# Attention within a chunk: scores from the diagonal on, the blocks left of it by transposing

## The chip, the cores and the metric

The kernel runs on one core of one Trainium2 chip. A core has a matrix engine (TensorE, PE in the profile; PEld is its weight load), a vector engine (VectorE, DVE), an engine for activation functions (ScalarE, ACT), a general one (GpSimd, POOL), and SyncE (SP), which issues transfers. They run side by side, each works through its own queue in order, and semaphores join them. The metric is the device time of one execution in microseconds, as the median of several runs.

## The reference

The program computes two layers on an input of 2 x 128 x 64 x 64. The first layer is a group norm, a neighbourhood attention and three linear layers. The second takes the image as 4096 tokens of 128 channels and adds an attention of the normalised tokens with themselves, and then a spectral filter layer. The change is in the attention of the second layer. Cut to what matters:

```python
def _L1_attn_ref(q):                       # q: 2 x 4096 x 128, the layer-normed tokens
    scale = 1.0 / np.sqrt(128)
    sim = jnp.einsum('blh,bmh->blm', q, q) * scale
    sim = jnp.where(eye, -1e9, sim)        # a token doesn't see itself
    attn = jax.nn.softmax(sim, axis=-1)
    return jnp.einsum('blm,bmh->blh', attn, q)

t = t + _L1_attn_ref(_ln_t(t))
```

Queries, keys and values are the same tensor, so the matrix of scores is symmetric, and so is the matrix of its exponentials, since no row maximum is taken off. Everything is in fp32.

## The kernel before, in words

Up to about 346 us the first layer runs. Then come the two batches of the second layer's attention, one after the other, and from about 1306 us the filter layer.

For a batch, `attention(b, fill)` (L882) divides the 4096 tokens into 8 chunks of 512, each of them four tiles of 128 tokens. `cm[b]` holds the normalised tokens with the channels on the partitions, `tok[b]` the same with the tokens on the partitions. Because of the symmetry only the 36 pairs of chunks (a, c) with c at or behind a are computed (`pairs`, L892). For a pair, `weights(a, c, k)` (L895) makes four tiles `e`, one for each tile k of chunk a, of 128 x 512 exponentials: one matmul into a PSUM bank (L899), in a diagonal pair (a = c) an addition of -1e6 on the diagonal of the tile's own 128 x 128 block by VectorE (L904), and the exponential on ScalarE (L906), which also writes the row sums to `part[:, n, c]`.

A tile e of a pair off the diagonal is used twice. As it stands it is the moving operand of a product with `tok` that adds to the output of chunk c (`other`, L952). And `turned` (L909) transposes its blocks, four to a bank (L913), and a VectorE instruction (L916) copies the bank to SBUF as `et` and sums its rows into `part[:, n, a]`; `et` is the moving operand of the product for chunk a (`own`, L927). In a diagonal pair the four tiles hold the full 512 x 512 square of exponentials, both of its triangles computed from scores, and only `own` is fed, with e itself.

The main loop (L938) goes through the pairs. In the four steps of a pair it issues the scores of the following pair (`weights(*following, j)`), the products of this one, one late product with an `et`, and one portion of other work by `fill()`: the end of the first layer, the token preparation of the second batch, filters, and for a finished chunk `after` (L969: transposing back, dividing by the sum over `part`, layer norm and the transform products L1012 and L1022) and `short_lags` (L1036, with L1053). In the second batch `fill()` also loads and mixes the filter matrices (`filter_matrices`, L1121; its loads of `st` land in two buffers, L1112, and VectorE consumes them at L1117 and L1119). The first scores of a batch (L937) are issued ahead of the loop, with no product between them.

Buffers around the change: PSUM has eight banks; `own` and `other` take one each, and six are handed out in turn by `bank()` (L865) for scores, transposes and fill work alike. Tiles `e` have eight buffers, tiles `et` four, `part` one.

What sets the order: each engine's queue is in order. Inside the blocks `with tc.manual_schedule(...)` (the first layer on four engines, the filter layer on PE) the order is as written. The attention stands in no such block, so there the framework's planner puts each engine's instructions in order: by the order of the program, and by when it expects inputs and buffers to be ready. A PE instruction whose input isn't there holds up everything behind it on PE.

Of the kernel before, what the change touches and what calls it, by code (L numbers as in the profile page):

```python
# [8 lines left out]
F32 = mybir.dt.float32  # L9
AF = mybir.ActivationFunctionType  # L10
ALU = mybir.AluOpType
# [3 lines left out]
P = 128  # L15
# [3 lines left out]
NT = T // P  # L19
# [8 lines left out]
ASCALE = P ** -0.5  # L28
# [58 lines left out]
CHUNKS = (0, 1, 4, 5, 2, 3, 6, 7)  # L87
# [8 lines left out]
def kernel(  # L96
# [16 lines left out]
    nc = tc.nc  # L113
# [18 lines left out]
    tt, tok, cm = [None, None], [None, None], [None, None]  # L132
# [11 lines left out]
    ident = const.tile([P, P], F32, name="ident")  # L144
# [79 lines left out]
    with l0a:  # L224
# [6 lines left out]
        sp = l0a.enter_context(tc.tile_pool(name="l0_s", bufs=2))  # L231
# [626 lines left out]
    with ap_:  # L858
        tp = ap_.enter_context(tc.tile_pool(name="l1_t", bufs=1, side="right"))
        ep = ap_.enter_context(tc.tile_pool(name="l1_e", bufs=8, side="right"))  # L860
        sp = ap_.enter_context(tc.tile_pool(name="l1_s", bufs=2, side="right"))
# [3 lines left out]
        def bank():  # L865
            return ps_m.tile([P, 512], F32, tag="bank", name="bank")
# [7 lines left out]
        one = tp.tile([P, 512], F32, name="one")  # L874
# [7 lines left out]
        def attention(b, fill):  # L882

            part = sp.tile([P, NT, 8], F32, tag="part", name="part", bufs=1)
            pairs = [(a, c) for a in range(8) for c in range(a, 8)]  # L892
            chunk = lambda a: slice(CHUNKS[a] * 512, (CHUNKS[a] + 1) * 512)

            def weights(a, c, k):  # L895

                n = 4 * CHUNKS[a] + k
                ps = bank()
                nc.tensor.matmul(  # L899
                    ps, lhsT=cm[b][:, n * P : (n + 1) * P], rhs=cm[b][:, chunk(c)], start=True, stop=True  # L900
                )
                if a == c:
                    ks = slice(k * P, (k + 1) * P)
                    nc.vector.tensor_tensor(ps[:, ks], ps[:, ks], ndiag, ALU.add)  # L904
                e = ep.tile([P, 512], F32, tag="e", name="e")
                nc.scalar.activation(e, ps, AF.Exp, bias=0.0, scale=ASCALE, accum_out=part[:, n, c : c + 1])  # L906
                return e

            def turned(a, c, m, es):  # L909

                pt = bank()
                for k in range(4):
                    nc.tensor.transpose(pt[:, k * P : (k + 1) * P], es[k][:, m * P : (m + 1) * P], ident)  # L913
                et = ep.tile([P, 512], F32, tag="et", name="et", bufs=4)
                n = 4 * CHUNKS[c] + m
                nc.vector.tensor_tensor_reduce(  # L916
                    et, pt, one, 1.0, 0.0, ALU.mult, ALU.add, part[:, n, a : a + 1]
                )
                return et

            own = None

            def onto(a, n, e, first, last):
                nonlocal own
                if first:
                    own = ps_o.tile([P, 512], F32, tag="own", name="own")
                nc.tensor.matmul(own, lhsT=tok[b][:, n, :], rhs=e, start=first, stop=last)  # L927
                if last:
                    xs = xa[b][:, chunk(a)]
                    if a:  # L930
                        nc.vector.tensor_tensor(xs, own, xs, ALU.add)
                    else:
                        nc.vector.tensor_copy(xs, own)
                    fill(CHUNKS[a], part)

            late = []
            es = [weights(0, 0, k) for k in range(4)]  # L937
            for i, (a, c) in enumerate(pairs):  # L938
                following = pairs[i + 1] if i + 1 < len(pairs) else None
                coming = []  # L940
                if a != c:
                    other = ps_o.tile([P, 512], F32, tag="other", name="other")
                for k in range(0, 4, 2):
                    for j in (k, k + 1):
                        if following:
                            coming.append(weights(*following, j))
                        if a == c:
                            while late:
                                onto(*late.pop(0))
                            onto(a, 4 * CHUNKS[a] + j, es[j], j == 0, a == 7 and j == 3)  # L950
                        else:
                            nc.tensor.matmul(  # L952
                                other, lhsT=tok[b][:, 4 * CHUNKS[a] + j, :], rhs=es[j], start=(j == 0), stop=(j == 3)
                            )
                        if late:
                            onto(*late.pop(0))
                        fill()
                    if a != c:
                        for j in (k, k + 1):
                            late.append((a, 4 * CHUNKS[c] + j, turned(a, c, j, es), False, c == 7 and j == 3))  # L960
                if a != c:
                    xs = xa[b][:, chunk(c)]
                    if a:
                        nc.vector.tensor_tensor(xs, other, xs, ALU.add)
                    else:
                        nc.vector.tensor_copy(xs, other)
                es = coming
# [223 lines left out]
        def filler(b, steps, kept=None):  # L1191

            urgent, done = [], []

            def fill(c=None, part=None):
                if c is not None:
                    done.append(c)
                    urgent.append(after(b, c, part))
                    if len(done) % 4 == 0:
                        held = kept if kept is not None and len(done) == 4 else urgent  # L1200
                        held.append(short_lags(b, len(done) // 4 - 1))
                    return

                for queue in (urgent, steps):
                    while queue:
                        got = next(queue[0], False)
                        if got is None:
                            return
                        if got:
                            break  # L1210
                        queue.pop(0)

            return fill, urgent
# [17 lines left out]
        steps = [drain(), chosen, filters(), tokens(1, bank)]  # L1231
        fill, left = filler(0, steps)
        attention(0, fill)
        for gen in steps:
            for _ in gen:
# [30 lines left out]
        kept = []  # L1266
        fill, left = filler(1, steps, kept)
        attention(1, fill)
        for gen in steps:
            for _ in gen:  # L1270
# [18 lines left out]
    with ExitStack() as cv:  # L1289
# [17 lines left out]
        def group():  # L1307


            y = cp.tile([P, 8, KF, 2, 32], F32, tag="y", name="y", bufs=2)  # L1310
            for q in range(GB // 2):
                ct, ut = ahead.pop(0)
                for par in range(2):

                    cv_ = ct[:, :, 0 : 288 + par * 32].rearrange("p o (l c) -> p o l c", l=2)[:, :, :, 0 : FB * KF]
                    for b in range(NB):
                        for f in range(2):
                            fp = slice(f * 64, (f + 1) * 64)
                            pc = ps_c.tile([P, 2, 2, FB * KF], F32, tag="pc", name="pc")
                            nc.tensor.matmul(pc, lhsT=ut[fp, b, par, :], rhs=cv_[fp], start=True, stop=True)  # L1320
                            (nc.scalar.copy if f else nc.vector.tensor_copy)(  # L1321
                                y[:, 4 * f : 4 * f + 4, :, par, b * 2 * FB + q : (b + 1) * 2 * FB : 2],
                                pc.rearrange("p r l (t k) -> p (r l) k t", k=KF),
                            )
                if to_load:
                    q_ = to_load.pop(0)
                    ahead.append((blocks(q_), inputs(q_)))
            return y
# [34 lines left out]
        with tc.manual_schedule(engines={mybir.EngineType.PE}):  # L1363
            y = group()
            for g in range(BINS // GB):
                following = group() if g + 1 < BINS // GB else None
# [17 lines left out]
        for b in range(NB):  # L1384
            for par in range(2):
                pt = ps_c.tile([P, 4, P], F32, tag="pc", name="pt")
# [5 lines left out]
        for h in range(2):  # L1392
            for b in range(NB):
                o = cp.tile([P, P, FB, 2], F32, tag="o", name="o", bufs=2)
                for par in range(2):
# [4 lines left out]
                    for i in range(4):  # L1400
                        for q, py in ((0, odd), (1, even)):
# [3 lines left out]
                                start=(q == 0), stop=(q == 0 or i == 3),  # L1405
# [102 lines left out]
```

## Time and profile before

| what | value |
|---|---|
| median of 3 runs | 2209.53 us (2209.5 to 2211.03) |
| profiled execution | 2211.93 us, its span 2210.2 us |
| PE busy | 2156.2 us, 98% of the span |
| DVE, ACT, POOL busy | 938.0, 780.6, 278.5 us |
| scores, L899 | 576 records, 297.9 us busy |
| exponentials, L906 | 288, 171.8 us busy, 597 ns each |
| transposes of e, L913 | 896 records, 117.2 us busy |
| copies with row sums, L916 | 224, 145.5 us busy, 687 ns each |
| diagonal additions, L904 | 64, 300 ns each (median) |

A fp32 matmul appears as two records on PE, each with a weight load; a transpose as one. A record's length runs into that of the next, since matmuls are pipelined, so what a matmul costs is read from start to start. In a row of the timeline stand the start, the length, the engine, the line, the operation, output and inputs, the shapes, how many records are merged, and in square brackets how long the engine was idle before it and what ended that.

### The profile page before, as it was taken

What the parts mean: (1) busy time and instruction counts of PE and PEld (TensorE: products, weight loads), DVE (VectorE), ACT (ScalarE), POOL (GpSimd) and SP (SyncE); (2) the same over time, 40 slices, a digit from 0 to 9 for tenths busy, and PEclk for the clock granted to TensorE, in tenths of its full rate; (3) what the DMA queues carried; (4) which work ended last, traced back from release to release, by engine and by line L of the source; (5) the groups of instructions that cost most, each with busy time, mean ns of one, the idle gap of its engine ahead of it and who ended that gap; (6) DMA issues with size and microseconds to landing.
All of it is one profiled execution on the core that took longest, in us unless ns stands there. A gap on an engine that the chain in (4) does not pass through costs nothing.

```text
span 2210.2 us, 31763 instructions
## 1 busy us (share of the span) xinstructions
PE 2156.2 (98%) x11920; PEld 1335.0 (60%) x11920; DVE 938.0 (42%) x3054; ACT 780.6 (35%) x1904; POOL 278.5 (13%) x355
## 2 busy tenths in 40 slices
PE   7899998999999998999999999999999999999998
PEld 4677765544554444544544447767767676777776
DVE  5899985434443346433333442232222323232232
ACT  3898883222333222222223232232222323232232
POOL 3477874200000000000000000000000000000000
PEclk8999999999999999999999999999999999999999
DMA  4222212021000025000000141221212121212101
GB/s 147 61 62 61 62 50 52 0 77 43 24 24 25 24 68 156 24 25 24 0 25 24 48 111 40 59 52 47 59 44 55 43 56 43 57 42 57 40 10 77
DMA packets 170345, 110.54 MB, mean 50 GB/s; under 512 B 21311, under 2 KB 155087, under 8 KB 169680
## 3 DMA queue, kind: packets, MB, share of 16 engines
q1 hardware_dynamic: 169266, 105.01, 17.8%
q8 instruction: 94, 1.54, 0.3%
q0 software_dynamic: 576, 2.10, 0.3%
q10 hardware_dynamic: 350, 1.41, 0.3%
q14 instruction: 59, 0.48, 0.1%
HBM read 73.86 MB, written 34.63 MB: 49 GB/s over the span
## 4 chain that ended last, share of the span: by engine, by line
PE 88%; DVE 5%; POOL 3%; DMA 2%; ACT 1%; issue 1%; SPq 1%; POOLq 0%; DVEq 0%; ACTq 0%
PE acc L1332 25%; PE pc L1320 13%; PE own L927 11%; PE bank L899 11%; PE other L952 8%; PE bank L913 4%; PE bank L333 2%; PE bank L1053 2%; PE bank L193 1%; PE bank L543 1%; PE bank L1012 1%; PE py L1354 1%; PE bank L507 1%; DMA st<-in_m_minus_dram 1%; PE po L565 1%; DVE ln_st L379 1%
## 5 line engine op out<-in xcount | busy, mean ns | idle before, releaser
L1321 DVE COPY y<-pc 128x512 f32<-128x512 f32 x320 | 221.6, 692 | 351.5 <-PE pc L1320 347.8
L906 ACT ACTIVATE e<-bank 128x512 f32<-128x512 f32 x288 | 171.8, 597 | 516.2 <-PE bank L899 387.8
L899 PE MATMUL bank<-cm 128*128 128x512 f32 x576 | 297.9, 601 | 1.4 <-DVE y L654 1.4
L1332 PE MATMUL acc<-y,mpl 128*128 128x256 f32 x1280 | 292.1, 382 | 0.0
L1332 PE MATMUL acc<-y,mmi 128*128 128x256 f32 x1280 | 288.0, 379 | 0.0
L1320 PE MATMUL pc<-ct,ut 64*128 64x512 f32 x1280 | 285.2, 595 | 0.9 <-issue 0.9
L1332 PEld LDWEIGHTS acc<-y,mpl 128*128 128x128 f32 x1280 | 238.1, 190 | 59.4 <-issue 29.6
L1332 PEld LDWEIGHTS acc<-y,mmi 128*128 128x128 f32 x1280 | 242.6, 190 | 32.6
L927 PE MATMUL own<-et,tok 128*128 128x512 f32 x448 | 228.5, 597 | 7.5 <-DVE part L916 7.4
L1321 ACT COPY y<-pc 128x512 f32<-128x512 f32 x320 | 205.1, 641 | 86.6 <-PE pc L1320 86.6
L952 PE MATMUL other<-e,tok 128*128 128x512 f32 x448 | 229.7, 594 | 0.0
L1320 PEld LDWEIGHTS pc<-ct,ut 64*128 64x128 f32 x1280 | 121.5, 187 | 145.8 <-issue 140.6
L916 DVE CUSTOM_DVE_ANT_0 et<-bank,one 128x512 f32<-128x512 f32 x224 | 145.5, 687 | 131.5 <-PE bank L913 131.4
L1339 ACT COPY ob<-acc 128x256 f32<-128x256 f32 x32 | 19.0, 595 | 387.0 <-PE acc L1332 387.0
L927 PEld LDWEIGHTS own<-et,tok 128*128 128x128 f32 x448 | 84.4, 191 | 117.5 <-issue 73.3
L952 PEld LDWEIGHTS other<-e,tok 128*128 128x128 f32 x448 | 85.2, 191 | 107.8 <-issue 106.0
L1356 DVE TENSOR_TENSOR xa<-py,xa 128x512 f32<-128x512 f32 x32 | 22.1, 692 | 281.4 <-PE py L1354 281.4
L913 PEld LDWEIGHTS bank<-ident,e 128*128 128x128 f32 x896 | 102.9, 141 | 55.4 <-issue 47.0
L899 PEld LDWEIGHTS bank<-cm 128*128 128x128 f32 x576 | 94.5, 191 | 67.9 <-issue 44.7
L165 POOL TENSOR_TENSOR ln_rs<-ln_rs,mhalf 128x4 f32<-128x4 f32 x24 | 24.5, 1020 | 837.1 <-DVE ln_rs L164 837.1
L530 ACT ACTIVATE p<-p,mn 128x196 f32<-128x196 f32 x256 | 114.4, 449 | 14.3 <-DVE mn L520 13.8
L913 PE MATMUL bank<-ident,e 128*128 128x128 f32 x896 | 117.2, 274 | 0.0
(210 smaller groups left out, 2289.3 us busy)
## 6 DMA issues: line engine op xcount, KB each, us to landing
ut<-us SPq DMA_DIRECT2D x80, 256.0 KB
us<-ub SPq DMA_DIRECT2D x64, 256.0 KB
vw<-vd SPq DMA_DIRECT2D x256, 49.0 KB
ct<-gs SPq DMA_DIRECT2D x160, 72.0 KB
ct<-gs SPq DMA_DIRECT2D x160, 64.0 KB
gs<-sum SPq DMA_DIRECT2D x20, 256.0 KB
vd<-v SPq DMA_DIRECT2D x128, 32.0 KB
st<-in_m_plus_dram SPq DMA_DIRECT2D x16, 256.0 KB
```

Source lines behind the costliest of these rows:

```text
L333: nc.tensor.matmul(pl, lhsT=wg[:, lo : lo + P], rhs=zT, start=True, stop=True)
L530: nc.scalar.activation(p, p, AF.Exp, bias=t[name + "mn"][:, h : h + 1], scale=-1.0, accum_out=t["den"][:, u, h : h + 1],)
L899: nc.tensor.matmul(ps, lhsT=cm[b][:, n * P : (n + 1) * P], rhs=cm[b][:, chunk(c)], start=True, stop=True)
L906: nc.scalar.activation(e, ps, AF.Exp, bias=0.0, scale=ASCALE, accum_out=part[:, n, c : c + 1])
L913: nc.tensor.transpose(pt[:, k * P : (k + 1) * P], es[k][:, m * P : (m + 1) * P], ident)
L916: nc.vector.tensor_tensor_reduce(et, pt, one, 1.0, 0.0, ALU.mult, ALU.add, part[:, n, a : a + 1])
L927: nc.tensor.matmul(own, lhsT=tok[b][:, n, :], rhs=e, start=first, stop=last)
L952: nc.tensor.matmul(other, lhsT=tok[b][:, 4 * CHUNKS[a] + j, :], rhs=es[j], start=(j == 0), stop=(j == 3))
L1053: nc.tensor.matmul(py, lhsT=mu[:, lag, :], rhs=zc[:, from_par, s0 : s0 + 512], start=(lag == 0), stop=(lag == 2))
L1320: nc.tensor.matmul(pc, lhsT=ut[fp, b, par, :], rhs=cv_[fp], start=True, stop=True)
L1321: (nc.scalar.copy if f else nc.vector.tensor_copy)(y[:, 4 * f : 4 * f + 4, :, par, b * 2 * FB + q : (b + 1) * 2 * FB : 2], pc.rearrange("p ...
L1332: nc.tensor.matmul(acc, lhsT=(mmi if l else mpl)[:, k, :], rhs=y[:, 1::2, k, ::-1, :] if l else y[:, 0::2, k, :, :], start=(l == 0 and k = ...
```

## The change

In a diagonal pair, the tile for k = 1, 2, 3 gets scores only from its own 128 x 128 block to the right: the matmul, the exponential and its row sum start at column `lo` = 128 k. The blocks left of it are the transposes of blocks that the pair's earlier tiles hold (`left`, the list of tiles made so far): k PE transposes into another bank, and one VectorE instruction copies them into e[:, 0:lo] and sums their rows into a ninth column of `part`, which is cleared once a batch by GpSimd. For k = 0 nothing changes but the size of `part`. Pairs off the diagonal stay as they were. Both callers hand over the list.

```diff
-            part = sp.tile([P, NT, 8], F32, tag="part", name="part", bufs=1)
+            part = sp.tile([P, NT, 9], F32, tag="part", name="part", bufs=1)
+            nc.gpsimd.memset(part[:, :, 8:9], 0.0)
             pairs = [(a, c) for a in range(8) for c in range(a, 8)]
...
-            def weights(a, c, k):
+            def weights(a, c, k, left=()):
 
                 n = 4 * CHUNKS[a] + k
+                lo = k * P if a == c else 0
                 ps = bank()
                 nc.tensor.matmul(
-                    ps, lhsT=cm[b][:, n * P : (n + 1) * P], rhs=cm[b][:, chunk(c)], start=True, stop=True
+                    ps[:, lo:], lhsT=cm[b][:, n * P : (n + 1) * P],
+                    rhs=cm[b][:, CHUNKS[c] * 512 + lo : (CHUNKS[c] + 1) * 512], start=True, stop=True,
                 )
                 if a == c:
                     ks = slice(k * P, (k + 1) * P)
                     nc.vector.tensor_tensor(ps[:, ks], ps[:, ks], ndiag, ALU.add)
                 e = ep.tile([P, 512], F32, tag="e", name="e")
-                nc.scalar.activation(e, ps, AF.Exp, bias=0.0, scale=ASCALE, accum_out=part[:, n, c : c + 1])
+                nc.scalar.activation(
+                    e[:, lo:], ps[:, lo:], AF.Exp, bias=0.0, scale=ASCALE, accum_out=part[:, n, c : c + 1]
+                )
+                if lo:
+                    pt = bank()
+                    for j in range(k):
+                        nc.tensor.transpose(pt[:, j * P : (j + 1) * P], left[j][:, lo : lo + P], ident)
+                    nc.vector.tensor_tensor_reduce(
+                        e[:, 0:lo], pt[:, 0:lo], one[:, 0:lo], 1.0, 0.0, ALU.mult, ALU.add, part[:, n, 8:9]
+                    )
                 return e
...
-            es = [weights(0, 0, k) for k in range(4)]
+            es = []
+            for k in range(4):
+                es.append(weights(0, 0, k, es))
...
-                            coming.append(weights(*following, j))
+                            coming.append(weights(*following, j, coming))
```

## The prediction

> **What bounds the kernel now.** I read the page's chain of waits first, then busy time by stretch over the attention, then the timeline of one step on the diagonal, then the rows that price the operations.
>
> The chain of waits:
>
> ```profile
> PE 88%; DVE 5%; POOL 3%; DMA 2%; ACT 1%; issue 1%; SPq 1%; POOLq 0%; DVEq 0%; ACTq 0%
> ```
>
> The end is set by TensorE (PE) nearly everywhere. Where it isn't shows in the busy time of PE, weight load, VectorE (DVE), ScalarE (ACT) and GpSimd (POOL) by stretch, with granted clock, DMA share and GB/s behind:
>
> ```profile
> 346.50:367.20 20.70, 18.87 (x61) 9.39 (x61) 12.93 (x60) 8.19 (x23) 15.46 (x18) 1.00 0.54 70
> 367.20:812.00 444.80, 443.64 (x1540) 219.00 (x1541) 182.65 (x612) 127.73 (x332) 29.30 (x32) 1.00 0.10 30
> 812.00:882.00 70.00, 62.44 (x201) 28.15 (x200) 46.81 (x128) 18.78 (x48) 2.31 (x2) 0.95 0.56 155
> 882.00:1260.00 378.00, 378.00 (x1271) 185.58 (x1270) 138.19 (x413) 102.35 (x276) 6.04 (x6) 1.00 0.09 25
> ```
>
> In 367 to 812 and 882 to 1260 PE is busy throughout and the chain names hardly anything but PE, so PE work saved there comes off the time. The first stretch (first batch starts) and the third (second batch starts) are different: the chain runs over transfers and DVE, e.g. these two pieces of it (start, length):
>
> ```profile
> 350.76 2.54 DMA st<-in_m_u_dram
> ...
> 818.51 3.23 DMA st<-in_m_plus_dram
> ```
>
> Each batch has eight diagonal pairs. By the times of the diagonal's DVE addition (L904), the first pair of each batch (348 and 818 us) lies in such a stretch, the other fourteen in the two PE stretches.
>
> One step on a diagonal, second batch, timeline (start, length):
>
> ```profile
> 1011.69 1.02 PE L899 MATMUL bank<-cm 128*128 128x512 f32 x2
> 1012.55 1.02 PE L952 MATMUL other<-e,tok 128*128 128x512 f32 x2
> 1012.75 0.30 DVE L904 TENSOR_TENSOR bank<-bank,ndiag 128x128 f32<-128x128 f32 x1
> 1013.14 0.60 ACT L906 ACTIVATE e<-bank 128x512 f32<-128x512 f32 x1 [3.10 <-DVE bank L904]
> 1013.41 1.02 PE L927 MATMUL own<-et,tok 128*128 128x512 f32 x2
> 1014.27 1.02 PE L899 MATMUL bank<-cm 128*128 128x512 f32 x2
> 1016.84 1.04 PE L913 MATMUL bank<-ident,e 128*128 128x128 f32 x8
> 1017.72 1.02 PE L899 MATMUL bank<-cm 128*128 128x512 f32 x2
> ```
>
> A fp32 product is two records. Start to start one of 512 columns takes 0.86 us (1011.69 to 1012.55); eight transposes take 0.88 (1016.84 to 1017.72). The e of the step is ready at 1013.74, 1.19 us after its score matmul's slot ended at 1012.55: 0.20 to DVE, 0.30 the addition, 0.09 to ACT, 0.60 the exponential.
>
> [...] here a 128-column transpose is 0.109 us and a 128-column product 0.222 (below), twice, and I use these. [...] L904 shows 0.30, used here.
>
> **The change part by part.**
>
> *Narrower scores.* Rows k = 1, 2, 3 of a diagonal pair compute 384, 256, 128 columns in place of 512. For 128 columns the nearest rows are the projection's four products, for 256 the later filter stage's 64 records of the chain:
>
> ```profile
> 355.67 1.05 PE L602 MATMUL bank<-w_sb,att 128*128 128x128 f32 x8
> 356.56 1.02 PE L899 MATMUL bank<-cm 128*128 128x512 f32 x2
> ...
> 1320.33 14.01 PE acc L1332 x64
> ```
>
> 0.89 / 4 = 0.222 us for 128 columns; 2 x 14.01 / 64 = 0.438 for 256; between them and 0.859, 0.648 for 384. Saved: 0.211 + 0.421 + 0.637 = 1.27 us a pair.
>
> *Turned left blocks.* 0 + 1 + 2 + 3 = 6 transposes at 0.109 = 0.66 us a pair. A lone transpose (k = 1) has no row of its own[...]. I take 0.109. Net on PE: 1.27 - 0.66 = 0.61 us a pair, and 14 x 0.61 = 8.6 us in the PE stretches.
>
> *ACT* loses 768 columns a pair. L906 at 512 is 0.597 us and ACT's 256-column copy (L1028) 0.374, so 0.87 ns a column: 0.67 us a pair, 11 in all, worth nothing while PE binds. It does bring e earlier.
>
> *DVE* gains three copies with sums a pair. L904's 0.30 at 128 and 0.687 of L916 at 512 give 0.30, 0.43, 0.56, plus three accumulator reads of 0.083: 1.54 us a pair, 24.6 in all. In the PE stretches DVE is busy 183 of 445 and 138 of 378 us, so this fits in idle time; the blocks are needed only when the diagonal's own products start, at least four score steps later. If that cover went (the addition of the next row late behind such a copy), ACT and then the transposes would be late.
>
> *The new wait.* The transposes of row k wait for e of row k - 1, and everything behind them on PE (products, fill work, later scores, thus ACT) waits too. In the fourteen pairs the gap from the end of an exponential to the next score matmul's start is 0.27 us at the least, typically 0.5 or 1.4 by turns, twice -0.04 (row 0 to row 1); the narrower matmul itself (0.65, 0.44, 0.22) comes before the transposes, so 0.6 us remain in nearly every case, against some 0.1 for the semaphore. Wait: nil, unless the order changes.
>
> *Banks.* Three more PSUM banks a pair from the six. One lives about 1 us (transposes, 0.2, copy), a score bank about 2, and a step lasts 2.6: room for both. Taken as nil; with fill work holding two more banks, up to 0.8 us a pair in the two pairs with transform products (7 and 15).
>
> *Memset* of the ninth column: one GpSimd instruction. It stands behind the 0.12 us memset of `zc` ahead of the first exponential (348.8), and at the second batch POOL is idle until 815. The row sums read 36 elements for 32. Both nil (at most 0.2).
>
> *The two first pairs.* PE savings don't count there; DVE additions may. First batch: DVE sits in the chain at 349.4 to 353.4, idle 0.96 and 0.68 us waiting for transfers. The first copy (0.38) with its wait falls before the instructions that free the next transfer's buffer, the rest into idle time: +0.8 us (0 to 1.6). Second batch: the same with the loads of m_plus, 1.48 us of idle DVE at 820 to 822: +0.5 (0 to 1.5).
>
> Sum: -8.6 + 0.8 + 0.5 = -7.3 us. The profiled execution took 2211.9 us (span 2210.2): 2204.6. The median of the runs is 2.4 below it; taking the same difference there, 2209.5 - 7.3 = 2202.2 us. The filter stage behind is PE throughout (877.5 of 878.2 us), so the shift is carried to the end.
>
> **Rivals.**
>
> *A. The gain is half lost in small waits* (banks, lone transposes, late DVE at the two starts): 0.25 a pair for 14 pairs, and 2.5 rather than 1.3 at the starts: -8.6 + 3.5 + 2.5 = -2.6, 2206.9. For it: DVE's copies stand between other work in a strict queue. Against: the slack above.
>
> *B. The transposes really wait: slower.* At both starts PE runs the four score matmuls in a row. If the order puts those of a pair so close in all fourteen, e of row 0 comes 1.29 us after its matmul (the 1.19 and 0.1 for the semaphore), with 0.65 covered: 0.64 lost; row 1's e is then in time; row 2's comes 1.07 after its matmul (addition, 256-column exponential), with 0.44 covered: 0.6 lost less the first transposes, say 0.4. Waits 1.05 against 0.61 gained: +0.44 a pair, +6.2, with the starts +7.5: 2217.0. It decides from a mean wait of 0.52 us a pair (no gain left). Against: two products separate the scores in all fourteen now, and PE's order here isn't written out but planned.
>
> *C. More is gained.* At the second start PE idles 4.42 us and then runs at half clock (two records 1.70 us apart from the next, not 0.86):
>
> ```profile
> 841.93 2.07 PE L927 MATMUL own<-et,tok 128*128 128x512 f32 x2 [4.42 <-DVE part L916]
> 844.65 1.91 PE L899 MATMUL bank<-cm 128*128 128x512 f32 x2
> 846.35 1.78 PE L952 MATMUL other<-e,tok 128*128 128x512 f32 x2
> ```
>
> This hangs on where DVE's queue stands, which the new copies shift. Without this wait some 6 us more: 2196. With it doubled, the gain would be gone.
>
> *D. It doesn't do what it says:* narrow products bound by their weight load. Two loads of 0.19 us for 128 columns, 0.38 and not 0.222, cost 0.16 a pair, 2.2 us: 2204.4. L602 speaks against it.
>
> **How the numbers follow.** Forecast with D's size: 0.60 (2199.5 to 2205); A 0.17; B 0.10; C 0.13. A difference under 0.2% (4.4 us) can't be told from none. Faster by more (below 2205.1): 0.60 + 0.12 = 0.72; slower (above 2213.9): 0.10; the same: 0.18. The range leaves out B, the edge of C and little of A: 2197 to 2210.
>
> **What would show it.** L899 in the diagonal pairs with three more forms, 8.6 to 10 us less start-to-start time in all; 96 transposes more from the new line, spaced 0.109; 48 copies of 0.30 to 0.56 us on DVE, 25 us with reads; no idle PE in front of the new transposes; the two PE stretches 4.3 us shorter each. Wrong if PE waits for e at the new transposes, if the second start lengthens, or if DVE's addition comes late and ACT after it.

## The result, and the profile after

| | before | after |
|---|---|---|
| median | 2209.78 us (6 runs, 2208.23 to 2211.52) | 2200.49 us (6 runs, 2199.01 to 2204.77) |
| span of the profiled execution | 2210.2 us | 2199.1 us |
| ratio of the times | | 0.9953, 95% interval 0.9943 to 0.9964 |

The change is faster by 0.47%, 9.3 us between the medians; 2202.2 was forecast. Two later comparisons of the same two kernels gave smaller differences, 8.1 and 7.5 us (below). The ratio of every run below is to the kernel before on the same chip, whose median there was 2209.9 to 2211.8 us.

The chain of waits after the change is as much a TensorE chain as before:

```profile
PE 89%; DVE 5%; POOL 3%; ACT 1%; DMA 1%; issue 1%; SPq 0%; POOLq 0%; DVEq 0%; ACTq 0%
```

The forecast's two PE stretches (in the columns it explains). The first is cut at the same work as before; it holds 42 more PE instructions, the six transposes of seven pairs, and is 441.0 us for 444.8, with PE idle 1.3 us in it for 1.2. The second is cut about half a microsecond too short; by the marks of the table below, 4.3 us came off there:

```profile
366.80:807.80 441.00, 439.68 (x1582) 221.84 (x1583) 189.18 (x654) 122.99 (x332) 29.41 (x33) 1.00 0.10 30
877.00:1250.00 373.00, 373.00 (x1310) 188.05 (x1309) 144.43 (x455) 97.58 (x276) 6.04 (x6) 1.00 0.09 25
```

One diagonal pair of the first batch in the timeline of PE (start, length):

```profile
443.80 0.81 PE L903 MATMUL bank<-cm 128*128 128x384 f32 x2
444.44 0.27 PE L917 MATMUL bank<-ident,e 128*128 128x128 f32 x1
444.55 1.02 PE L968 MATMUL other<-e,tok 128*128 128x512 f32 x2
...
447.15 0.60 PE L903 MATMUL bank<-cm 128*128 128x256 f32 x2
447.58 0.38 PE L917 MATMUL bank<-ident,e 128*128 128x128 f32 x2
447.80 1.02 PE L968 MATMUL other<-e,tok 128*128 128x512 f32 x2
...
449.52 0.38 PE L903 MATMUL bank<-cm 128*128 128x128 f32 x2
449.74 0.49 PE L917 MATMUL bank<-ident,e 128*128 128x128 f32 x3
450.07 1.02 PE L968 MATMUL other<-e,tok 128*128 128x512 f32 x2
```

From start to start the narrow scores take 0.64, 0.43 and 0.22 us in place of 0.86, and one, two and three transposes 0.11, 0.22 and 0.33. No row has a bracket: nothing here waited. The next two views show the one kind of place where PE did wait for an exponential, and the new work on DVE. First two of the waits of PE between 345 and 1310 us (us in total, times, longest); the 2.3 us at the new transposes are two waits, 1.25 and 1.04 us, one in the first pair of each batch:

```profile
PE own L941 <- DVE part L930: 6.4, 7, 3.6
...
PE bank L917 <- ACT e L911: 2.3, 2, 1.2
```

Then the groups of DVE by form (busy us, mean ns of one), 24.0 us in all, for which 24.6 were forecast:

```profile
L918 DVE CUSTOM_DVE_ANT_0 e<-bank,one 128x384 f32<-128x384 f32 x16 | 8.9, 556 | 0.3
L918 DVE CUSTOM_DVE_ANT_0 e<-bank,one 128x256 f32<-128x256 f32 x16 | 6.6, 415 | 0.0
L918 DVE CUSTOM_DVE_ANT_0 e<-bank,one 128x128 f32<-128x128 f32 x16 | 4.5, 281 | 1.1 <-PE bank L917 1.1
L918 DVE DVE_READ_ACCUMULATOR2_ANT part<- 128x1 f32 x48 | 4.0, 83 | 0.0
```

**Where the time went, step by step.** The first PE transpose that brings a finished chunk back (L976 before, L992 after) marks the same work in both traces, sixteen times, once for each chunk of a batch. The table has how much earlier or later each stretch between such marks became against before, in three profiled executions of the changed kernel (the last two from the runs below):

| stretch | after | after_again | e11_after_beside |
|---|---|---|---|
| up to the first score | -0.74 | -0.78 | -1.47 |
| first pair of batch 0 (first score to first `own` with `et`) | +0.39 | +0.04 | -0.01 |
| seven inner pairs of batch 0 | -3.89 | -3.85 | -3.90 |
| second start (seventh mark to the 17th product of `own` with `et` in batch 1) | -0.68 | -0.06 | +1.42 |
| seven inner pairs of batch 1 | -4.31 | -4.30 | -4.29 |
| the last pair's end | -1.59 | 0.00 | -1.60 |
| filter layer and tail | -0.34 | -0.33 | -0.32 |
| span | -11.15 | -9.28 | -10.17 |

The inner pairs give 8.2 us in each of the three, within 0.05. The other lines differ by up to 2.1 us between executions of one kernel. The last pair's end is a stretch of PE at half clock that some executions have there and others don't (last section). Ahead of the first score PE has the same 4514 instructions in all fourteen profiles, and yet the first score starts at 343.7 to 349.4 us; PE is without work there for 15.4 to 19.4 us from 28 us on in the two at the ends of this range. Why was not tried. The filter layer and tail are 0.3 to 0.4 us shorter in every other profile than in the one of before, also in that with only the first pairs changed.

### The profile page after: what moved, and what is told of

It is laid out like the page before. It is cut to its first block, busy times and chain, and to the rows that moved or that the text cites. A ratio compares the mean times of both kernels' runs of the same rounds, so it can differ in the third digit from the quotient of the medians.

```text
span 2199.1 us, 32064 instructions
## 1 busy us (share of the span) xinstructions
PE 2145.5 (98%) x12016; PEld 1341.3 (61%) x12016; DVE 952.8 (43%) x3150; ACT 769.9 (35%) x1904; POOL 278.7 (13%) x357
## 4 chain that ended last, share of the span: by engine, by line
PE 89%; DVE 5%; POOL 3%; ACT 1%; DMA 1%; issue 1%; SPq 0%; POOLq 0%; DVEq 0%; ACTq 0%
PE acc L1348 25%; PE pc L1336 13%; PE own L941 11%; PE bank L903 10%; PE other L968 8%; PE bank L927 4%; PE bank L333 2%; PE bank L1069 2%; PE bank L543 2%; PE bank L193 2%; PE bank L1028 1%; PE py L1370 1%; PE bank L507 1%; PE po L565 1%; ACT p L530 1%; POOL ln_rs L387 1%
## 5 line engine op out<-in xcount | busy, mean ns | idle before, releaser
L911 ACT ACTIVATE e<-bank 128x512 f32<-128x512 f32 (+3 forms) x288 | 161.6, 561 | 513.9 <-PE bank L903 396.7
L903 PE MATMUL bank<-cm 128*128 128x512 f32 (+3 forms) x576 | 278.4, 565 | 1.4 <-DVE y L654 1.4
```

The costliest lines, as they stand in the source:

```text
L903: nc.tensor.matmul(ps[:, lo:], lhsT=cm[b][:, n * P : (n + 1) * P], rhs=cm[b][:, CHUNKS[c] * 512 + lo : (CHUNKS[c] + 1) * 512], start=True, ...
L911: nc.scalar.activation(e[:, lo:], ps[:, lo:], AF.Exp, bias=0.0, scale=ASCALE, accum_out=part[:, n, c : c + 1])
```

## The experiments

### The changed kernel once more

> The changed kernel once more, to separate what belongs to the change from what one profiled execution happens to show. Column theory (the gain is TensorE columns in the fourteen inner diagonal pairs): median near 2200.5, 0.995 to 0.9965 of before, and again 0.61 us less per inner diagonal pair in the trace. What lay outside those pairs in the first profile (0.74 us ahead of the attention, 1.5 us behind the last pair) need not come back: if it does, it is an effect of the change that the forecast missed; if it doesn't, it is the chance of one execution.

Measured: 2201.82 us (2200.36 to 2203.69), ratio to before 0.9962 (0.995 to 0.9975). The 1.5 us that the last pair had seemed to give are not in its profile (table above). They were not the change's.

### The transposes left out

```diff
-                    pt = bank()
-                    for j in range(k):
-                        nc.tensor.transpose(pt[:, j * P : (j + 1) * P], left[j][:, lo : lo + P], ident)
                     nc.vector.tensor_tensor_reduce(
-                        e[:, 0:lo], pt[:, 0:lo], one[:, 0:lo], ...
+                        e[:, 0:lo], one[:, 0:lo], one[:, 0:lo], ...
```

The blocks left of the diagonal then hold ones; that part of the computation is left out.

> The narrower scores stay, the 96 transposes go (the copy into the left blocks reads a tile of ones from SBUF, so the left blocks hold ones: this part of the computation is left out). Column theory: the transposes cost 0.66 us of TensorE in each of the fourteen inner pairs, so 9.2 us under the changed kernel, about 2191.3. Relief theory (the gain comes from ScalarE's shorter exponentials and earlier tiles, TensorE's columns hide): no change, about 2200.5. If the transposes also hold TensorE up by waiting, more than 9.2 comes off.

Measured: 2196.79 us (2191.64 to 2198.58), ratio 0.9939 (0.9925 to 0.9952), profiled span 2189.9. Inside the trace each inner pair but one gains 1.27 to 1.31 us on before, where the change gains 0.61 to 0.65: 0.66 more, six transposes at 0.11, one for one. But the median lies only 5.0 us below the changed kernel's on the same chip, where 14 x 0.66 = 9.2 had been due. Hence a second run of the same kernel:

> The same kernel as e1_no_turn (the six transposes of a diagonal pair left out; the copies read a tile of ones, so the blocks left of the diagonal hold ones and that part of the computation is left out). There one profiled execution was 2191.6 us, while the median was 2196.8. By start-to-start times the 96 transposes are 10.5 us, of which 84 x 0.109 = 9.2 lie in the inner pairs: if they come off the time one for one, the median is 2191 to 2193. If the idle time that their absence makes costs TensorE half-clock stretches of 3.4 us in most executions, each worth 1.7 us, the median is 2195 to 2198 again, and the mean granted clock of the slower executions is lower than that of the faster.

Measured: 2195.57 us (2192.3 to 2197.63), ratio 0.993 (0.9918 to 0.9942), profiled span 2195.4. This time the profiled execution was one of the longer ones, 5.5 us above the first, so the two profiles can be compared. Busy time by stretch of the second profile, at two of the places where TensorE ran at half clock (the granted clock is the third number from the end):

```profile
78.32:81.73 3.41, 3.41 (x51) 2.85 (x57) 2.19 (x5) 2.45 (x6) 2.94 (x6) 0.50 0.24 55
...
1255.91:1259.33 3.42, 3.42 (x11) 1.41 (x12) 0.69 (x1) 1.75 (x3) 0.00 (x0) 0.50 0.00 0
```

and the same stretches of the first:

```profile
78.32:81.73 3.41, 2.68 (x60) 2.05 (x60) 2.76 (x6) 3.41 (x10) 3.13 (x6) 1.00 0.24 55
...
1255.91:1259.33 3.42, 3.42 (x15) 1.82 (x12) 0.88 (x3) 1.35 (x3) 0.00 (x0) 1.00 0.76 224
```

Between the kernel's start-up and its end the second profile has 20.5 us at half clock, the first 10.2. Half of the difference would be 5.1 us, but the places don't bear it out one by one: 3.5 of the 5.5 us lie before the first score, where the second has one stretch of 3.41 us more and PE is also without work 3.0 us longer (18.4 us for 15.4, from 28 us on), 0.5 at the second start and 1.6 at the last pair, where the stretch at 1255.91 alone makes the difference. So executions of one kernel differ by such stretches, and by idle time ahead of the attention.

The record also has the mean granted clock of each of these executions. In the second run the three longer executions (2195.6 to 2197.6 us) had 0.990 and 0.991 and the two shorter ones (2192.3 and 2193.2) 0.994, as was expected if half clock makes the difference. Half clock doesn't explain the shortfall, though. By the mean of the ten executions (2195.4) against the sixteen of the change (2201.9) the transposes cost 6.4 us and not 9.2; the mean clocks of the two groups are 0.9923 and 0.9927, and in the 121 executions whose clock is on record, compared within one kernel on one chip, a clock lower by 0.001 goes with 1.1 us more, so that this accounts for about half a microsecond. From the first `own` with `et` to the last marked transposes but one, the two profiles are 16.8 and 16.3 us shorter than before, those of the change 8.9, 8.2 and 6.8. So the profiles show 8.6 us of the 9.2 and the times 6.4. The remainder stays open; what a transpose costs on PE is not in doubt.

### Full-width scores, all else as changed

```diff
-                    ps[:, lo:], lhsT=..., rhs=cm[b][:, CHUNKS[c] * 512 + lo : (CHUNKS[c] + 1) * 512], ...
+                    ps, lhsT=..., rhs=cm[b][:, CHUNKS[c] * 512 : (CHUNKS[c] + 1) * 512], ...
```

> Transposes and shorter exponentials stay, the score matmuls of the diagonal pairs are 512 columns wide again (the extra columns are computed and not used). Column theory: 1.27 us more in each of fourteen pairs, 17.8 us over the changed kernel and 8.5 to 9.2 over the kernel before, about 2218.5 to 2219. Relief theory: the gain stays, about 2200.5.

Measured: 2220.30 us (2218.8 to 2221.69), ratio 1.0046 (1.0033 to 1.0058). Its PE timeline has the score of 512 columns in front of the transposes, 0.86 us start to start:

```profile
446.84 1.02 PE L903 MATMUL bank<-cm 128*128 128x512 f32 x2
447.70 0.27 PE L917 MATMUL bank<-ident,e 128*128 128x128 f32 x1
447.81 1.02 PE L968 MATMUL other<-e,tok 128*128 128x512 f32 x2
```

Each inner pair is 0.64 to 0.67 us longer than before (one 0.71). So the gain is in the columns of the matmul: with them, ACT's shorter exponentials remain and buy nothing, and the transposes alone make the kernel slower. From full width to narrow a pair goes from +0.66 to -0.61, that is 1.27, the first term of the forecast's sum to the digit.

### The copies doubled

```diff
+                    for _ in range(2):
                       nc.vector.tensor_tensor_reduce(
```

> Each copy of a left block on VectorE is issued twice, 24.6 us of VectorE work more. If the copies are hidden as the forecast took them: 2200.5 within 1.5 us, the rise coming from the first pair of each batch alone (0.8 and 0.5 us forecast for one set of copies). If the cover is thin (half-lost-gain rival), a good part of the 24.6 us shows: 2205 or more.

Measured: 2202.89 us (2201.13 to 2204.79), ratio 0.9966 (0.9954 to 0.9979), against 2201.82 and 0.9962 for the changed kernel on the same chip. The median is 0.9 us above the range set down for hidden copies and well below the 2205 for a thin cover; from the changed kernel beside it the time can't be told. 24 us more of DVE work in the attention leave no mark on the inner pairs, which still give 0.61 to 0.65 us, the second again less (0.15). What the work does is lengthen the waits of PE for DVE's `et`, from 6.4 us in seven places to 10.2 in ten; those that are longer or new all lie in the second start and just behind it (837 to 897 us). A cost of a microsecond or two there can't be excluded: the mean granted clock of these executions was higher, 0.9934 for 0.9926.

### Scores of a diagonal pair issued in a row

```diff
+                        if following and following[0] == following[1]:
+                            while j == 0 and len(coming) < 4:
+                                coming.append(weights(*following, len(coming), coming))
-                        if following:
+                        elif following:
                             coming.append(weights(*following, j, coming))
```

> All four score matmuls of a diagonal pair are issued in the first step of the pair before, with nothing between them in the program. Rival B (the transposes wait for the exponential where the scores stand close): waits of 1.05 us in each of fourteen pairs, some 2215 to 2217 with the starts. Column theory with a planner that fills such gaps: it puts other products between the narrow scores and the transposes, so waits of 0.1 us a pair at most, 2199 to 2203.

Measured: 2203.33 us (2202.73 to 2207.31), ratio 0.9967 (0.9955 to 0.9979). PE in its trace, from the scores of rows 0 and 1 (merged in the first line) to the last new transpose, the same pair as above:

```profile
439.83 1.67 PE L903 MATMUL bank<-cm 128*128 128x512 f32 x4
441.33 1.02 PE L971 MATMUL other<-e,tok 128*128 128x512 f32 x2
442.19 0.27 PE L917 MATMUL bank<-ident,e 128*128 128x128 f32 x1
442.30 0.60 PE L903 MATMUL bank<-cm 128*128 128x256 f32 x2
442.74 0.38 PE L917 MATMUL bank<-ident,e 128*128 128x128 f32 x2
442.95 0.39 PE L903 MATMUL bank<-cm 128*128 128x128 f32 x2
443.18 0.38 PE L917 MATMUL bank<-ident,e 128*128 128x128 f32 x2
443.40 1.02 PE L941 MATMUL own<-et,tok 128*128 128x512 f32 x2
444.26 0.27 PE L917 MATMUL bank<-ident,e 128*128 128x128 f32 x1
```

and the waits of PE for an exponential:

```profile
PE bank L917 <- ACT e L911: 2.3, 2, 1.2
```

So the four scores of each inner pair did move close together, with a single product between them, and the planner put another in front of the last transpose: the order of PE isn't quite the program's. That was enough: the only waits at the new transposes are the change's own, in the two first pairs. In rival B's terms, row 0's tile comes 1.29 us after its matmul, and now 0.64 us of score and 0.86 of one product cover it. B's case, with nothing between, was not brought about in the inner pairs; it stands in the two first pairs, where no product stands between the scores of rows 0 and 1 and the first transpose, and PE waits 1.25 and 1.04 us, where B had put 1.05 a pair. The new order cost something else: the inner pairs give 6.0 us in place of 8.2. The last one of each batch, where the planner also split the transform products, is 0.8 us longer than in the change, and the second of batch 0 has a wait of 0.63 us for an `et`.

### Only the inner pairs, only the first pairs

```diff
-                lo = k * P if a == c else 0
+                lo = k * P if a == c and a else 0          # inner pairs only
+                lo = k * P if a == c and not a else 0      # first pairs only
```

> The change in the fourteen inner diagonal pairs alone; the first pair of each batch is as before. Forecast: the first pairs cost 1.3 us, so 1.3 under the changed kernel, about 2199.2. Reading of the changed kernel's trace: the first pair of the first batch costs 0.4 us, that of the second nothing, so 2200.1. Both: 8.6 us under before, so the whole gain is in these pairs. If the first pairs hold a part of the gain, 2202 or more.

Measured: 2202.56 us (2200.37 to 2204.92), ratio 0.9961 (0.9949 to 0.9973).

> The change in the first diagonal pair of each batch alone. Forecast: 1.3 us slower than before, about 2211. Reading of the changed kernel's trace: 0.2 to 0.4 slower, about 2210. If the first pairs give TensorE's 0.61 us each like the others: 2208.6.

Measured: 2210.30 us (2207.09 to 2211.4), ratio 0.999 (0.9982 to 0.9998); the inner pairs of its trace are within 0.02 us of before, but for one (+0.11, the second of batch 0).

The fourteen inner pairs alone give what the change gives, by the ratios; the absolute times of these two runs are not to be held against those expected, as the kernel before took 2211.78 us on this chip. No cost of the two first pairs shows: the first pair of batch 0 is 0.01 us longer in the trace than before, and the forecast's +1.3 us would be a ratio of 1.0006, outside the interval. The ratio alone would be weak evidence, since the mean granted clock was 0.9934 in these executions and 0.9922 in those of the kernel before.

### The second start: loads spread, then the layer norm held back

Rival C hung on the 4.42 us in which PE idles at the second start, with half clock after it. The change left it standing, 0.8 us shorter. PE in the trace after, then DVE:

```profile
837.48 2.07 PE L941 MATMUL own<-et,tok 128*128 128x512 f32 x2 [3.62 <-DVE part L930]
```

```profile
834.33 0.48 DVE L1133 TENSOR_SCALAR mpl<-st,wt 128x512 f32<-128x512 f32 x1
835.71 1.11 DVE L182 TENSOR_SCALAR z<-tt,ln_mv,ln_rs 128x128 f32<-128x128 f32 x4 [0.90 <-POOL ln_rs L165]
836.74 0.68 DVE L930 CUSTOM_DVE_ANT_0 et<-bank,one 128x512 f32<-128x512 f32 x1
```

The `et` copy starts at 836.74, though the transposes it reads were done at about 832.1. Two causes were possible: DVE late because its mixing steps wait for the transfers of `st`, or because of the layer norm that stands ahead of the copy in its queue. The first was tried by spreading the mixing over four steps of the loop for each matrix group, one load waited for in each while the next is in flight:

```diff
+        def mixed_apart(dst, src):
+            ahead_ = [load(0)]
+            for i in range(NBR):
+                if i + 1 < NBR:
+                    ahead_.append(load(i + 1))
+                yield
+                ...                                   # mix ahead_.pop(0) as before
...
-                    mixed(dst[:, k0 : k0 + 4, :], src[:, k0 : k0 + 4])
-                    yield
+                    yield from mixed_apart(dst[:, k0 : k0 + 4, :], src[:, k0 : k0 + 4])
```

> The changed kernel, with the mixing of the filter matrices in the second batch spread: one load is waited for in a step of the main loop, the next one in flight, in place of four loads in one step. If the 3.6 us wait of TensorE at the second start and the half clock behind it come from VectorE's queue standing at these loads: both go, and the waits of 0.5 us behind them, together 6 to 8 us, 2192.5 to 2194.5. If the second start is bound by something else (the transposing of the new blocks, the token preparation): 2200.5 within 1.5.

Measured: 2201.51 us (2200.26 to 2204.65), ratio 0.9958 (0.9946 to 0.997). The stall is still there:

```profile
836.34 2.08 PE L941 MATMUL own<-et,tok 128*128 128x512 f32 x2 [3.26 <-DVE part L930]
```

This does not settle the first cause, for the edit did not reach DVE: in its trace DVE's instructions from 800 to 898 us are, one by one, those of the changed kernel in the same order. The planner put the mixing where it had been, with its waits for `st` ahead of the copy (1.51, 1.70 and 0.70 us, for 1.17, 2.08 and 0.59).

The second was tried by holding back the leftovers of batch 0 by six steps, so that their layer norm can't stand ahead of the copy (the pause stands ahead of the filter matrices too, but in the trace their mixing stays ahead of the copy):

```diff
+        def pause(n):
+            for _ in range(n):
+                yield
+
-        steps = [*left, filter_matrices(mpl, mmi), load_blocks()]
+        steps = [pause(6), *left, filter_matrices(mpl, mmi), load_blocks()]
```

> The change, and at the second start the leftover work of the first batch's last two chunks (transposing back, layer norm, transform products) is held back by six steps of the loop; nothing is left out. In the change's profile the first copy of a turned block of the second batch starts at 836.74 us, though its transposes were done at 832.1: about 4 us of layer norm, with a wait for GpSimd in it, stand ahead of it in VectorE's queue. If that queue makes the stall (3.62 us idle on PE, then 3.4 to 6.8 us at half clock, which cost half their length), the copy starts within 1 us of its transposes, the idle time is under 0.8 us, the half clock is gone, and the time is 5 to 6 us below the change: 2194.5 to 2196, the profiled span about 2194. If the queue isn't what counts, because the held back layer norm and its transform products make a stall as long a few microseconds later, the time stays at 2200 to 2202 with a new wait of over 2 us between 840 and 875 us.

Measured: 2201.06 us (2196.64 to 2201.73), ratio 0.9956 (0.9943 to 0.997), profiled span 2194.9. The stall in its trace, and two more, shorter, in the following 20 us (1.30 and 0.26); then the copy:

```profile
828.96 1.13 PE L941 MATMUL own<-et,tok 128*128 128x512 f32 x2 [0.67 <-DVE part L930]
```

```profile
828.21 0.68 DVE L930 CUSTOM_DVE_ANT_0 et<-bank,one 128x512 f32<-128x512 f32 x1
```

With the layer norm behind the copy, 3.62 us of idle PE became 0.67, and there was no half clock at the second start. That and the profiled span came as expected for this case; but the copy still starts 1.6 us after its transposes and not within 1, and the median is 2201.06 and not 2196 or less. The profiled execution was the lowest of five, so the run was repeated with the changed kernel beside it:

> e8_norm_later once more, with the changed kernel beside it on the same chip. In its profile the idle time of 3.62 us and the half clock at the second start were gone and the span was 2194.9 us, but the other four executions took 2199.5 to 2201.7. If the stall at the second start is worth its 4 to 6 us in every execution, this kernel's median is at least 3 us below that of the changed kernel in this run. If what it saves there is lost at other places, or is within what the half-clock stretches of TensorE vary by, the medians are within 1.5 us of each other; the profile should then show half-clock stretches of 3.4 us where the first profile had none.

> The changed kernel itself, unaltered, as the other side of that comparison: 2200 to 2202 by its two earlier medians (2200.5 and 2201.8), with about 3.6 us of idle TensorE and half clock after it at the second start, 0.61 us less per inner diagonal pair than before, and 0.1 to 0.2 for the second pair.

Measured: 2199.62 us (2196.62 to 2204.31), ratio 0.9954 (0.9941 to 0.9967), against 2202.53 us (2201.76 to 2203.6), ratio 0.9966 (0.9952 to 0.9979), for the changed kernel. In the repeat the stall is reduced less, and a second one follows:

```profile
833.11 1.13 PE L941 MATMUL own<-et,tok 128*128 128x512 f32 x2 [1.40 <-DVE part L930]
...
843.41 1.13 PE L941 MATMUL own<-et,tok 128*128 128x512 f32 x2 [1.54 <-DVE part L930]
```

Again there is no half clock at the second start, but 13.7 us of it elsewhere, where the first profile had 3.4. So the layer norm, with what went behind the copy together with it, made most of the stall. The copy still comes 1.6 and 2.4 us after its transposes; what stands ahead of it now is the mixing with its waits for `st`, whose share no run took apart.

From the first `own` with `et` to the last marked transposes of the attention but one, the two profiles with the layer norm held back are 12.8 and 11.7 us shorter than before, the three of the change 8.9, 8.2 and 6.8: some 4 us. The executions show less: the mean of ten is 2200.1 and that of sixteen of the change 2201.9, and their ranges overlap. That removing the stall makes the kernel faster was not shown: the difference in the times is 1.7 us by these means and 2.9 by the medians of the last comparison, where at least 3 had been set as the sign, and below what the intervals separate.

## Why the prediction was right, and where it wasn't

**Narrower scores, 1.27 us a pair:** right. The three matmuls take 0.22, 0.43 and 0.64 us less, 1.29 by the timeline, 1.27 by the step from full-width to narrow. Rival D (weight load binds) fell: 128 columns take 0.22 us, not 0.38.

**Transposes, 0.66 us a pair:** right, the lone one included: 0.11 us from start to start, though the weight load of a transpose is 0.14 us long in the trace. Rival A's 0.25 a pair, the author's estimate, didn't come from them. Net 0.61 a pair, as forecast.

**Fourteen inner pairs, -8.6 us:** measured -8.2 in each of three profiles. The missing 0.45 is one pair, the second inner pair of batch 0, which gives 0.16 us. There the step that DVE's work "fits in idle time" failed, because DVE isn't idle at that place. From 548 to 554 us it prepares tokens of batch 1 (layer-norm sums, a wait for GpSimd, four scalings) and only then copies the `et` that PE's `own` needs. The start of this chain, the copy and the product in the timeline of DVE and PE before:

```profile
549.10 0.29 DVE L174 BATCH_NORM_STATS2 ln_st<-tt 128x6 f32<-128x128 f32 x1
...
553.90 0.69 DVE L916 CUSTOM_DVE_ANT_0 et<-bank,one 128x512 f32<-128x512 f32 x1
```

```profile
555.00 1.88 PE L927 MATMUL own<-et,tok 128*128 128x512 f32 x4
```

and after:

```profile
548.21 0.41 DVE L918 CUSTOM_DVE_ANT_0 e<-bank,one 128x256 f32<-128x256 f32 x1
548.55 0.48 DVE L174 BATCH_NORM_STATS2 ln_st<-tt 128x6 f32<-128x128 f32 x2
...
552.99 0.68 DVE L930 CUSTOM_DVE_ANT_0 et<-bank,one 128x512 f32<-128x512 f32 x1
```

```profile
552.53 1.02 PE L903 MATMUL bank<-cm 128*128 128x512 f32 x2
553.74 1.98 PE L941 MATMUL own<-et,tok 128*128 128x512 f32 x4 [0.18 <-DVE part L930]
```

Before, the copy ended at 554.59 and PE came to it at 555.00, without a wait. After, PE was through with the score in front (552.53 and 0.86) at 553.39, 1.6 us earlier, but the copy started only 0.9 earlier. Part of this is that PE caught up with DVE's chain, part that the new copy for k = 2 (0.41 us and its read) and an addition stand ahead of the chain: it begins 0.55 us earlier than before (548.55 for 549.10), the work ahead of it 1.1. It is rival A's mechanism, at one place out of fourteen. How the two parts share the 0.45 isn't settled: with the copies doubled the pair still gave 0.15, without the transposes 0.36 of 1.27, and no run changed one of the two alone.

**The new wait, nil:** right for the fourteen; at the two first pairs PE did wait for an exponential, 2.3 us in all, where no product stands between the scores. The forecast named such a wait as a sign of being wrong and had said that savings of PE don't count in these two pairs; its sum had no wait there. Rival B decides from 0.52 us a pair; measured was zero in the pairs that count.

**Banks and memset, nil:** right for the banks by the pairs named: the last inner pair of each batch, with transform products beside it, gives 0.62 and 0.61. The memset takes 0.15 us on GpSimd, at 335.8 and 805.0 us, ahead of each batch.

**The two first pairs, +0.8 and +0.5:** too large. In three profiles +0.39, +0.04 and -0.01, and -0.68, -0.06 and +1.42 (the start of batch 1 with its stall in it, and in the last a further stall of 3.1 us at 857 us); with only these pairs changed, batch 0's was +0.01. The step that failed put a copy's length on the path to the next transfer. DVE is busy only 13.95 of the 21.0 us of the first start after the change, for 12.93 of 20.7 before, so idle time could take the copies up, as the lower bound of 0 had allowed; that this is the reason was not tried by itself.

**ACT and DVE, worth nothing:** right. Full-width scores with ACT's gain kept were slower than before by the whole transposes; doubled copies cost nothing in the inner pairs and nothing that the comparison of the times can tell.

**Rival C:** the wait did move, from 4.42 us to 3.62, 3.4 and 3.9 in three profiles, but did not vanish: what stands ahead of the copy in DVE's queue is layer norm and mixing. The forecast was right that it hangs on DVE's queue. What part the new copies have stays open: with the first pairs as before the wait is 4.42 and 4.75 us in two profiles, with them changed 2.89 to 3.93 in six, with the copies doubled 4.34.

The sum -7.3 was made of -8.6 and +1.3; the traces have -8.2 and, on average, +0.4. The two misses, 0.4 us too much gain and 0.9 too much cost, half cancel: the mechanism was right, but that the total came so near is partly luck. Three comparisons of the times gave -9.3, -8.1 and -7.5.

## What to carry to other kernels

On a matmul-bound stretch with fp32 operands, half of a symmetric block is worth replacing by transposes where a transpose costs half of the product of the same columns (here 0.11 us for 0.22 at 128 columns); count net start-to-start time, per pair, and take nothing for the other engines' relief. Before multiplying by the number of places, ask at each place how close the next engine is behind: the one where DVE was 0.4 us ahead of PE gave a quarter of the others' gain. And mark the same work in both traces: a difference of spans (11.2 us) held 3 us that the change hadn't made.

## What the runs showed of the hardware

Between start-up and end TensorE ran at half clock (granted clock 0.50) in stretches of 3.41 or 6.83 us, so at the second start (6.83 us from 841.05 us before, from 836.66 after), and how many a kernel gets changed from one execution to the next: the three profiles of the changed kernel had 17.1, 23.9 and 13.7 us of them, that of before 17.1. A stretch of 3.41 us in which PE is busy throughout cost about half its length: the last pair's -1.59 us in two of three profiles, against a gain of 9.3 for the whole change, is one that before had at 1271.1 us and these had not. Where PE idles in it, it cost less (0.5 us for one more at the second start, above). In the profiles of before and after the starts lie whole lengths of a stretch apart: those of before at 315.40 and 335.88 us are 20.48 us apart, six times 3.41, the next two follow after 148 and 126 times that length, and after the change those at 78.91, 314.42 and 836.66 us are 69 and 153 times apart. Why was not shown.

As for idle time, half clock came with it at the second start: where PE idles 4.42 us (before), 3.62 (after), 3.26 (loads spread) and 3.93 (the changed kernel beside the last run) in one piece, a stretch at half clock begins in that idle time or right behind it, and the score that follows takes 1.70 us from start to start in place of 0.86; in the two profiles with the layer norm held back, where no wait there is longer than 1.54 us, none does, and the scores take 0.86 to 0.97. That idle time sets it off was not shown: the 6.83 us from 314.42 us after the change have no wait of PE over 0.45 us in the 14 us ahead. A microsecond or two in one profile, away from the place that was changed, is no evidence.
